# Expert stage of an attention-plus-MoE layer: explicit program order, other stage distances, and the residual moved between engines

## The chip, the cores and the metric

The kernel runs on one core of one Trainium2 chip. A core has five engines with their own instruction queues: PE (TensorE, matrix multiplies and transposes, writes to PSUM), DVE (VectorE), ACT (ScalarE), POOL (GpSimd, which also issues the indirect DMAs) and SP (SyncE, which here issues the plain DMAs). The metric is the device time of the whole program in microseconds (us).

## The reference, cut to what matters

```python
x = x + layernorm(attention(layernorm(x)))          # x: 16 x 512 x 128, relative positions, 16 heads
x = x + layernorm(ffn(layernorm(x)))

def ffn(x):                                         # x: 8192 tokens x 128
    logits = x @ w_router.T                         # 16 experts, one is chosen
    mask = one_hot(top_1(logits)); scores = sigmoid(logits) * mask
    masked_inputs = scores.T[:, :, None] * x        # zero where the expert wasn't chosen
    gate, up = split(masked_inputs @ gate_up_proj)  # 128 -> 2 x 256, each expert's own weights
    expert_out = (up * silu(gate)) @ down_proj      # 256 -> 128
    shared = (silu(x @ w_gate.T) * (x @ w_up.T)) @ w_down.T
    return shared + expert_out.sum(over experts)
```

All values are float32.

## The kernel before, in words

The program has two stages. The attention stage goes through 16 batches of 512 tokens in 256 steps of 16 per batch; the order of its work on each engine is written out by hand, with every instruction pinned behind the one traced before it on the same engine (the class `InOrder`, whose calls all show up in the profile as L47). One job of this stage is `route` (L566): for the batch that has just been finished it forms `pay`, a row of 133 words for each token: 128 words of the residual stream x, then the mean and the reciprocal standard deviation of x (columns D and D+1), the router's score (D+2), the expert (D+3) and the token's own number (D+4). An indirect DMA on POOL puts each row where its expert's tokens are gathered, in the DRAM tensor `rows`. `route` for batch 0 to 14 runs its wide work on POOL, and for the last batch on DVE; it is a generator, and a few of its steps are taken in each attention step.

The expert stage (from L812) takes the gathered rows in blocks of 128 tokens, all of one expert. In this run 73 blocks are processed; a conditional part at the end would process up to six more. Each block i goes through these helpers:

- `fetch(i)` (L852): SP reads the expert's number from the row and loads its weights: `gu` (256 KB, L862) and `dn` (128 KB, L864), from a pool of four buffers each. Every eight blocks it first loads the next eight blocks of rows, `xc` (L837), and POOL computes the row numbers for the output, `to` (L840).
- `turn_in(i)` (L868): DVE normalises x with the stored mean and reciprocal (L872), ACT multiplies the result with the score (L875), PE transposes both (L878), ACT copies the two transposes out of PSUM (`xT`, L880).
- `gates(i)` (L883): 16 matmuls (L889), eight with the shared weights `wgu` and eight with the expert's `gu`; each eight are four for gate and up, two chunks each. ACT takes the sigmoid of the gates (L891), DVE multiplies it by the gate (L892) and by the up half (L894), which gives `h`.
- `leave(i)` (L897): eight matmuls `po` (L904) add the shared and the expert's down product in one PSUM tile. DVE takes mean and variance (L85, L86), adds epsilon (L78), POOL takes the power -1/2 (L80, `lf_rs`), DVE normalises (L909), POOL adds the residual (L910) and issues the indirect DMA that writes the rows to the output (L912).

`run` (L917) calls `fetch(i+3)`, `turn_in(i+1)`, `gates(i)`, `leave(i-1)` in each iteration. In this stage nothing is pinned except SP's fetches: the framework's scheduler chooses the order on each engine, subject to the data. The tiles x2, xT, g, h and f have three buffers each; the gates' PSUM tile has two, `po` has two and the transposes' has two.

Of the kernel before, what the change touches and what calls it, by code (L numbers as in the profile page):

```python
# [9 lines left out]
F32 = mybir.dt.float32  # L10
I32 = mybir.dt.int32
AF = mybir.ActivationFunctionType
ALU = mybir.AluOpType
# [4 lines left out]
P = 128  # L18
S = 512
D = 128  # L20
# [10 lines left out]
FF = 256  # L31
# [19 lines left out]
def relative_attention_then_moe(  # L51
# [6 lines left out]
    nc = tc.nc  # L58
# [7 lines left out]
    ident = const.tile([P, P], F32, name="ident")  # L66
# [8 lines left out]
    def rstd_of(pool, mv, n, tag, eng, root=nc.gpsimd):  # L75

        ve = pool.tile([P, n], F32, tag=f"{tag}_ve", name=f"{tag}_ve")
        eng.tensor_scalar_add(ve, mv[:, :, 1], EPS)  # L78
        rs = pool.tile([P, n], F32, tag=f"{tag}_rs", name=f"{tag}_rs")
        root.tensor_tensor(rs, ve, mhalf[:, 0:n], ALU.pow)  # L80
        return rs

    def stats(pool, mv, src, tag, eng):
        st = pool.tile([P, 6], F32, tag=f"{tag}_st", name=f"{tag}_st")
        eng.bn_stats(st, src)  # L85
        eng.bn_aggr(mv, st)  # L86

    def own_rows(group, dma):

        tc.declare_no_dep(dma.ins, group=group, reason="rows of their own")  # L90
        tc.add_to_no_dep_group(group, dma.ins)


    with ExitStack() as actx:
# [4 lines left out]
        sp = actx.enter_context(tc.tile_pool(name="attn_small", bufs=4))  # L99
# [4 lines left out]
        pe, act, dve, sp_q, pool = (InOrder(tc, e) for e in (nc.tensor, nc.scalar, nc.vector, nc.sync, nc.gpsimd))  # L104
# [461 lines left out]
        def route(b, c0=0, c1=NC):  # L566
# [5 lines left out]
            nc_, pieces, nm = c1 - c0, slice(c0, c1), f"{b}_{c0}"  # L572
# [3 lines left out]
            rs = rstd_of(sp, mvy, nc_, "ry", dve, pool)  # L576
            if b == B - 1:
                yield
            pay = bp.tile([P, nc_, PW], F32, tag="pay", name=f"pay{nm}")
            pint = pay.bitcast(I32)  # L580
            mv = sp.tile([P, nc_, 2], F32, tag="mv1", name=f"mv1_{nm}")
# [13 lines left out]
            rs1 = rstd_of(sp, mv, nc_, "l1", dve, pool)  # L595
# [3 lines left out]
            for t in range(nc_):  # L599
                eng.tensor_scalar(  # L600
                    x2[:, t, :], pay[:, t, 0:D], mv[:, t, 0:1], rs1[:, t : t + 1], ALU.subtract, ALU.mult
                )
            pool.tensor_copy(pay[:, :, D : D + 1], mv[:, :, 0:1])
            pool.tensor_copy(pay[:, :, D + 1 : D + 2], rs1.unsqueeze(2))
            yield
            x2T = bp.tile([P, nc_ * P], F32, tag="x2T", name=f"x2T{nm}", bufs=1)
# [205 lines left out]
    with ExitStack() as fctx:  # L812
        wp = fctx.enter_context(tc.tile_pool(name="ffn_w", bufs=1))
        xp = fctx.enter_context(tc.tile_pool(name="ffn_x", bufs=1))
        ep = fctx.enter_context(tc.tile_pool(name="ffn_e", bufs=4))
        fp = fctx.enter_context(tc.tile_pool(name="ffn", bufs=3))
        sp = fctx.enter_context(tc.tile_pool(name="ffn_small", bufs=4))
        ps_g = fctx.enter_context(tc.tile_pool(name="ps_g", bufs=2, space=PSUM))
        ps_x = fctx.enter_context(tc.tile_pool(name="ps_x", bufs=2, space=PSUM))
        ps_f = fctx.enter_context(tc.tile_pool(name="ps_f", bufs=2, space=PSUM))  # L820

        wgu = wp.tile([P, 2 * FF], F32, name="wgu")
        wd = wp.tile([P, 2, D], F32, name="wd")
        nc.scalar.dma_start(wgu[:, 0:FF], w_gateT)
        nc.scalar.dma_start(wgu[:, FF : 2 * FF], w_upT)
        nc.scalar.dma_start(wd, w_downT.rearrange("(c p) o -> p c o", p=P))


        starts = [0, 2] + list(range(8, SURE, 8)) + [SURE, NBLK]
        rows_v = rows.rearrange("(n p) w -> p n w", p=P)  # L830
        row_of = {}
        ids_of = {}

        def fetch_rows(c):
            n0, n1 = starts[c], starts[c + 1]
            xc = xp.tile([P, n1 - n0, PW], F32, name=f"xc{c}")
            st["fetched"] = nc.sync.dma_start(xc, rows_v[:, n0:n1, :]).ins  # L837

            to = xp.tile([P, n1 - n0], I32, name=f"to{c}")
            nc.gpsimd.tensor_scalar(  # L840
                to.unsqueeze(2), xc[:, :, D + 4 : D + 5].bitcast(I32), -1.0, float(FAR), ALU.mult, ALU.add
            )
            for n in range(n0, n1):
                row_of[n] = xc[:, n - n0, :]
                ids_of[n] = to[:, n - n0 : n - n0 + 1]

        out_rows = out.rearrange("b s d -> (b s) d")
        gate_up_v = gate_up.rearrange("e p f -> p e f")
        down_v = down.rearrange("e (c p) o -> p e c o", p=P)
        st = {}  # L850

        def fetch(i):  # L852

            for c in range(2, len(starts) - 2):
                if starts[c - 1] == i:
                    with tc.issue_after(st["fetched"]):
                        fetch_rows(c)
            x = row_of[i]
            with tc.issue_after(st["fetched"]):
                e = nc.sync.value_load(x[0:1, D + 3 : D + 4].bitcast(I32), min_val=0, max_val=NE - 1)  # L860
            gu = ep.tile([P, 2 * FF], F32, tag="gu", name=f"gu{i}")
            nc.sync.dma_start(gu.unsqueeze(1), gate_up_v[:, bass.ds(e, 1), :])  # L862
            dn = ep.tile([P, 2, D], F32, tag="dn", name=f"dn{i}")
            last = nc.sync.dma_start(dn.unsqueeze(1), down_v[:, bass.ds(e, 1), :, :])  # L864
            st["fetched"] = last.ins
            st[i] = {"x": x, "gu": gu, "dn": dn}

        def turn_in(i):  # L868

            x = st[i]["x"]  # L870
            x2 = fp.tile([P, 2, D], F32, tag="x2", name=f"x2b{i}")
            nc.vector.tensor_scalar(  # L872
                x2[:, 0, :], x[:, 0:D], x[:, D : D + 1], x[:, D + 1 : D + 2], ALU.subtract, ALU.mult
            )
            nc.scalar.mul(x2[:, 1, :], x2[:, 0, :], x[:, D + 2 : D + 3])  # L875
            pt = ps_x.tile([P, 2, P], F32, tag="x", name=f"ptb{i}")
            for k in range(2):
                nc.tensor.transpose(pt[:, k, :], x2[:, k, :], ident)  # L878
            xT = fp.tile([P, 2, P], F32, tag="xT", name=f"xTb{i}")
            nc.scalar.copy(xT, pt)  # L880
            st[i]["xT"] = xT

        def gates(i):  # L883

            xT = st[i]["xT"]
            pg = ps_g.tile([P, 2, 4, P], F32, tag="g", name=f"pg{i}")
            for k, w in enumerate((wgu, st[i]["gu"])):
                for c in range(4):
                    nc.tensor.matmul(pg[:, k, c, :], w[:, c * P : (c + 1) * P], xT[:, k, :], start=True, stop=True)  # L889
            g = fp.tile([P, 2, 2, P], F32, tag="g", name=f"g{i}")  # L890
            nc.scalar.activation(g, pg[:, :, 0:2, :], AF.Sigmoid)  # L891
            nc.vector.tensor_mul(g, g, pg[:, :, 0:2, :])  # L892
            h = fp.tile([P, 2, 2, P], F32, tag="h", name=f"h{i}")
            nc.vector.tensor_mul(h, g, pg[:, :, 2:4, :])  # L894
            st[i]["h"] = h

        def leave(i):  # L897

            s = st.pop(i)
            x, h = s["x"], s["h"]  # L900
            po = ps_f.tile([P, D], F32, tag="f", name=f"po{i}")
            for k, w in enumerate((wd, s["dn"])):
                for c in range(2):
                    nc.tensor.matmul(po, h[:, k, c, :], w[:, c, :], start=(k == c == 0), stop=(k == c == 1))  # L904
            mv = sp.tile([P, 1, 2], F32, tag="mvf", name=f"mvf{i}")
            stats(sp, mv[:, 0, :], po, "lf", nc.vector)
            rs = rstd_of(sp, mv, 1, "lf", nc.vector)
            f = fp.tile([P, D], F32, tag="f", name=f"f{i}")
            nc.vector.tensor_scalar(f, po, mv[:, 0, 0:1], rs, ALU.subtract, ALU.mult)  # L909
            nc.gpsimd.tensor_add(f, f, x[:, 0:D])  # L910
            to = ids_of[i]
            own_rows("out", nc.gpsimd.indirect_dma_start(  # L912
                out_rows, bass.IndirectOffsetOnAxis(ap=to, axis=0), f, None,
                bounds_check=B * S - 1, oob_is_err=False,
            ))

        def run(i0, i1):  # L917

            for i in range(i0, min(i0 + 3, i1)):
                fetch(i)  # L920
            turn_in(i0)
            for i in range(i0, i1 + 1):
                if i + 3 < i1:
                    fetch(i + 3)
                if i + 1 < i1:
                    turn_in(i + 1)
                if i < i1:
                    gates(i)
                if i > i0:
                    leave(i - 1)  # L930

        for c in range(2):
            fetch_rows(c)
        run(0, SURE)

        opened = nc.values_load(blocks[0:1, 0:1], min_val=1, max_val=NBLK)
        with tc.If(opened > SURE):
            fetch_rows(len(starts) - 2)
            run(SURE, NBLK)
# [31 lines left out]
```

## Time and profile before

| | |
|---|---|
| three timed runs | 1972.97, 1973.37, 1974.53 us (median 1973.37) |
| the profiled execution | 1977.44 us, of which the span of instructions is 1975.7 us |
| busy over the span | PE 1905.7 us (96%), DVE 1539.5 (78%), ACT 1154.3 (58%), POOL 901.3 (46%) |
| mean granted clock of PE | 0.989 of full speed |
| attention stage | 0 to about 1730 us of the span |
| expert stage | about 1735 us to the end; last indirect DMA issued at 1970.32 us |

A page of the profile lists busy time for each engine, 40 slices of the span, the chain of work that ended last, and groups of equal instructions with their mean duration and with the idle time of their engine just before them, together with what ended that idle time. The timeline lists instructions in order of time. Each line starts with start and duration in us. "Busy" of PE counts the modelled ends of pipelined matmuls, so a PE that is always busy need not be issuing at its highest rate.

### The profile page before, as it was taken

Reading aid. Unit: us, or ns where it says so; the run is one execution under the profiler, and the core shown is the slowest. Engines: PE = TensorE matmul, PEld = TensorE weight load, DVE = VectorE, ACT = ScalarE, POOL = GpSimd, SP = SyncE. Lnnn points to the kernel's source line nnn. Section 1 sums busy time; section 2 is a strip of 40 time slices with the busy share of each in tenths; the row PEclk is TensorE's granted clock in tenths of the full one; section 3 lists DMA queues with packets and bytes.
Section 4 is the critical chain, followed back from the end, with each engine's and each line's share of the span. In section 5 each row is a group of like instructions: output and inputs, shape, how many; then the busy total and the mean of one; then the engine's idle time right before and its main releaser. Section 6 shows DMA issues by size and latency. Waiting matters only on the chain.

```text
span 1975.7 us, 92844 instructions
## 1 busy us (share of the span) xinstructions
PE 1905.7 (96%) x41070; PEld 1518.6 (77%) x41070; DVE 1539.5 (78%) x3922; ACT 1154.3 (58%) x2929; POOL 901.3 (46%) x1007
## 2 busy tenths in 40 slices
PE   6999999999999999999999999999999999689997
PEld 3777777777777777777777777777777777589997
DVE  4677787888787878787878888787878787757776
ACT  3666566666656666666666666666666666234432
POOL 4234454444444453535453544444444534246666
PEclk9999999999999999999999999999999999889999
DMA  2312000000000000000000000000000000066553
GB/s 75 69 30 42 14 23 5 14 14 6 22 5 24 5 23 3 25 3 25 3 25 3 25 3 16 12 12 16 5 18 5 18 7 5 13 176 176 173 165 95
DMA packets 88342, 68.94 MB, mean 35 GB/s; under 512 B 26439, under 2 KB 74340, under 8 KB 87808
## 3 DMA queue, kind: packets, MB, share of 16 engines
q1 hardware_dynamic: 81248, 53.60, 10.5%
q0 software_dynamic: 4384, 8.57, 1.2%
q8 instruction: 323, 5.29, 1.1%
q10 hardware_dynamic: 2304, 0.80, 0.2%
q14 instruction: 83, 0.68, 0.1%
HBM read 44.79 MB, written 18.75 MB: 32 GB/s over the span
## 4 chain that ended last, share of the span: by engine, by line
PE 80%; POOL 8%; DVE 6%; issue 5%; ACT 1%; DMA 1%; POOLq 0%; ACTq 0%; DVEq 0%; SPq 0%
PE ps L47 27%; PE pt L47 24%; PE pa L47 13%; PE pz L47 7%; POOL out_dram L912 4%; DVE nmax L47 3%; POOL lf_rs L80 2%; PE prt L47 2%; PE py L47 2%; POOL f L910 2%; PE pq L47 1%; PE pl L47 1%; PE pv L47 1%; PE pk L47 1%; DVE wT L47 1%
## 5 line engine op out<-in xcount | busy, mean ns | idle before, releaser
L47 ACT ACTIVATE w<-ps,nmax 128x512 f32<-128x512 f32 x1024 | 699.3, 693 | 497.7 <-DVE nmax L47 497.7
L47 DVE TENSOR_REDUCE nmax<-ps 128x1 f32<-128x512 f32 x1024 | 656.2, 683 | 288.3 <-PE ps L47 288.3
L47 PE MATMUL pt<-ident,w 128*128 128x128 f32 x4096 | 590.8, 280 | 3.1 <-DVE wT L47 2.7
L47 PEld LDWEIGHTS pt<-ident,w 128*128 128x128 f32 x4096 | 446.5, 141 | 139.0 <-issue 98.7
L47 ACT COPY wT<-pt 128x512 f32<-128x512 f32 x512 | 299.9, 586 | 129.0 <-PE pt L47 129.0
L47 DVE COPY wT<-pt 128x512 f32<-128x512 f32 x512 | 349.3, 682 | 1.6 <-PE pt L47 1.5
L47 PE MATMUL ps<-kT,qb 32*128 32x288 f32 (+10 forms) x4864 | 327.1, 375 | 5.4 <-POOL qb L47 3.8
L47 PE MATMUL pa<-wT,v 128*32 128x128 f32 x8192 | 276.7, 276 | 2.0 <-ACT R L47 1.2
L47 PE MATMUL ps<-relk,qr 64*32 64x288 f32 (+4 forms) x8192 | 275.2, 377 | 0.0
L47 PEld LDWEIGHTS ps<-kT,qb 32*128 32x128 f32 x4864 | 208.9, 186 | 62.9 <-issue 35.3
L47 PEld LDWEIGHTS pa<-wT,v 128*32 128x32 f32 x8192 | 208.0, 109 | 44.3 <-issue 41.6
L47 POOL TENSOR_TENSOR Rh<-R,mh 128x512 f32<-128x512 f32 x64 | 66.5, 1039 | 357.7 <-ACT R L47 351.2
L47 ACT ACTIVATION_READ_ACCUMULATOR w<-ps,nmax 128x1 f32 x1024 | 212.5, 208 | 0.0
L47 PEld LDWEIGHTS ps<-relk,qr 64*32 64x32 f32 x8192 | 124.4, 106 | 112.8 <-issue 82.8
L47 PE MATMUL pz<-wT,relv 128*32 128x48 f32 (+1 forms) x12288 | 192.1, 210 | 1.3 <-issue 1.3
L47 PEld LDWEIGHTS pz<-wT,relv 128*32 128x32 f32 x12288 | 184.1, 110 | 1.9 <-issue 1.9
L47 POOL TENSOR_TENSOR qr<-qz,mq 128x1024 f32<-128x1024 f32 x64 | 137.7, 2152 | 0.0
L47 POOL TENSOR_SCALAR kT<-kT,kend 128x512 f32<-128x512 f32 x32 | 49.8, 1562 | 145.0 <-ACT sg L47 128.3
L47 DVE TENSOR_REDUCE oT<-od 128x32 f32<-128x128 f32 x256 | 97.6, 381 | 8.9
L875 ACT ACTIVATE x2b<-x2b,xc 128x128 f32<-128x128 f32 x73 | 29.0, 401 | 125.2 <-DVE lf_ve L78 114.0
L47 POOL COPY rb<-rt 128x512 f32<-128x512 f32 x64 | 39.0, 609 | 116.6 <-DVE rt L47 104.7
L47 POOL DMA_INDIRECT rows<-pay,at_i x64 | 68.0, 1062 | 51.9 <-DVE shift L47 41.4
(157 smaller groups left out, 2241.8 us busy)
## 6 DMA issues: line engine op xcount, KB each, us to landing
gu<-_L_ffn_gate_up_proj_dram SPq DMA_DIRECT2D x73, 256.0 KB
dn<-in_L_ffn_down_proj_dram SPq DMA_DIRECT2D x73, 128.0 KB
rows<-zero SPq DMA_DIRECT2D x19, 266.0 KB
xc<-rows SPq DMA_DIRECT2D x8, 532.0 KB
x_sb<-in_L_attn_x_dram SPq DMA_DIRECT2D x64, 64.0 KB
qd<-qp SPq DMA_DIRECT2D x16, 256.0 KB
qz<-qd SPq DMA_DIRECT2D x248, 16.0 KB
relv<-vext SPq DMA_DIRECT2D x1, 1536.0 KB
```

The costliest lines, as they stand in the source:

```text
L47: return lambda *a, **k: self.tc.keep_in_program_order(op(*a, **k))
L80: root.tensor_tensor(rs, ve, mhalf[:, 0:n], ALU.pow)
L875: nc.scalar.mul(x2[:, 1, :], x2[:, 0, :], x[:, D + 2 : D + 3])
L910: nc.gpsimd.tensor_add(f, f, x[:, 0:D])
L912: own_rows("out", nc.gpsimd.indirect_dma_start(out_rows, bass.IndirectOffsetOnAxis(ap=to, axis=0), f, None, bounds_check=B * S - 1, oob_is ...
```

## The change

The edits lie in the expert stage, except for one in `route`.

- Every PE, ACT, DVE and POOL instruction of the helpers is now pinned in program order, with the same class as in the attention stage. SP's loads and the small POOL instruction `to` stay as they were.
- `route` stores minus mean times reciprocal in column D, computed by DVE, where POOL copied the mean.
- `norm(i)` is a helper of its own. ACT does both its instructions: x times the reciprocal plus column D, and then the product with the score.
- `gates(i)` orders its 16 matmuls as the gates of both layers first and the ups after them; the PSUM tile is laid out the same way, so the eight gates lie together. The two products are in `product(i)`.
- The down product, its statistics and the POOL power are in `down_proj(i)`, called two blocks behind the gates. `leave(i)`, called three behind, has DVE form `nm` (minus mean times reciprocal), ACT form x plus `nm` (`xb`), DVE form po times the reciprocal plus `xb` (f), and POOL issue the output DMA. The separate POOL addition is gone.
- The weights' pool has six buffers and the working tiles have four.
- The order of an iteration is: fetch(i+3), leave(i-3), turn_in(i+1), norm(i+2), gates(i), product(i), down_proj(i-2).

```diff
@@ -600,7 +600,9 @@
                 eng.tensor_scalar(
                     x2[:, t, :], pay[:, t, 0:D], mv[:, t, 0:1], rs1[:, t : t + 1], ALU.subtract, ALU.mult
                 )
-            pool.tensor_copy(pay[:, :, D : D + 1], mv[:, :, 0:1])
+            dve.scalar_tensor_tensor(
+                pay[:, :, D : D + 1], mv[:, :, 0:1], -1.0, rs1.unsqueeze(2), ALU.mult, ALU.mult
+            )
             pool.tensor_copy(pay[:, :, D + 1 : D + 2], rs1.unsqueeze(2))
             yield
             x2T = bp.tile([P, nc_ * P], F32, tag="x2T", name=f"x2T{nm}", bufs=1)
@@ -812,12 +814,13 @@
     with ExitStack() as fctx:
         wp = fctx.enter_context(tc.tile_pool(name="ffn_w", bufs=1))
         xp = fctx.enter_context(tc.tile_pool(name="ffn_x", bufs=1))
-        ep = fctx.enter_context(tc.tile_pool(name="ffn_e", bufs=4))
-        fp = fctx.enter_context(tc.tile_pool(name="ffn", bufs=3))
+        ep = fctx.enter_context(tc.tile_pool(name="ffn_e", bufs=6))
+        fp = fctx.enter_context(tc.tile_pool(name="ffn", bufs=4))
         sp = fctx.enter_context(tc.tile_pool(name="ffn_small", bufs=4))
         ps_g = fctx.enter_context(tc.tile_pool(name="ps_g", bufs=2, space=PSUM))
         ps_x = fctx.enter_context(tc.tile_pool(name="ps_x", bufs=2, space=PSUM))
         ps_f = fctx.enter_context(tc.tile_pool(name="ps_f", bufs=2, space=PSUM))
+        pe, act, dve, pool = (InOrder(tc, e) for e in (nc.tensor, nc.scalar, nc.vector, nc.gpsimd))
 
         wgu = wp.tile([P, 2 * FF], F32, name="wgu")
         wd = wp.tile([P, 2, D], F32, name="wd")
@@ -865,52 +868,70 @@
             st["fetched"] = last.ins
             st[i] = {"x": x, "gu": gu, "dn": dn}
 
-        def turn_in(i):
+        def norm(i):
 
             x = st[i]["x"]
             x2 = fp.tile([P, 2, D], F32, tag="x2", name=f"x2b{i}")
-            nc.vector.tensor_scalar(
-                x2[:, 0, :], x[:, 0:D], x[:, D : D + 1], x[:, D + 1 : D + 2], ALU.subtract, ALU.mult
-            )
-            nc.scalar.mul(x2[:, 1, :], x2[:, 0, :], x[:, D + 2 : D + 3])
+            act.activation(x2[:, 0, :], x[:, 0:D], AF.Identity, bias=x[:, D : D + 1], scale=x[:, D + 1 : D + 2])
+            act.mul(x2[:, 1, :], x2[:, 0, :], x[:, D + 2 : D + 3])
+            st[i]["x2"] = x2
+
+        def turn_in(i):
+
             pt = ps_x.tile([P, 2, P], F32, tag="x", name=f"ptb{i}")
             for k in range(2):
-                nc.tensor.transpose(pt[:, k, :], x2[:, k, :], ident)
+                pe.transpose(pt[:, k, :], st[i]["x2"][:, k, :], ident)
             xT = fp.tile([P, 2, P], F32, tag="xT", name=f"xTb{i}")
-            nc.scalar.copy(xT, pt)
+            act.copy(xT, pt)
             st[i]["xT"] = xT
 
         def gates(i):
 
             xT = st[i]["xT"]
-            pg = ps_g.tile([P, 2, 4, P], F32, tag="g", name=f"pg{i}")
-            for k, w in enumerate((wgu, st[i]["gu"])):
-                for c in range(4):
-                    nc.tensor.matmul(pg[:, k, c, :], w[:, c * P : (c + 1) * P], xT[:, k, :], start=True, stop=True)
+            pg = ps_g.tile([P, 2, 2, 2, P], F32, tag="g", name=f"pg{i}")
+            for u in range(2):
+                for k, w in enumerate((wgu, st[i]["gu"])):
+                    for c in range(2):
+                        a = u * FF + c * P
+                        pe.matmul(pg[:, u, k, c, :], w[:, a : a + P], xT[:, k, :], start=True, stop=True)
             g = fp.tile([P, 2, 2, P], F32, tag="g", name=f"g{i}")
-            nc.scalar.activation(g, pg[:, :, 0:2, :], AF.Sigmoid)
-            nc.vector.tensor_mul(g, g, pg[:, :, 0:2, :])
+            act.activation(g, pg[:, 0], AF.Sigmoid)
+            st[i].update(pg=pg, g=g)
+
+        def product(i):
+
+            pg, g = st[i]["pg"], st[i]["g"]
+            dve.tensor_mul(g, g, pg[:, 0])
             h = fp.tile([P, 2, 2, P], F32, tag="h", name=f"h{i}")
-            nc.vector.tensor_mul(h, g, pg[:, :, 2:4, :])
+            dve.tensor_mul(h, g, pg[:, 1])
             st[i]["h"] = h
 
-        def leave(i):
-
-            s = st.pop(i)
-            x, h = s["x"], s["h"]
+        def down_proj(i):
+
+            s = st[i]
+            h = s["h"]
             po = ps_f.tile([P, D], F32, tag="f", name=f"po{i}")
             for k, w in enumerate((wd, s["dn"])):
                 for c in range(2):
-                    nc.tensor.matmul(po, h[:, k, c, :], w[:, c, :], start=(k == c == 0), stop=(k == c == 1))
+                    pe.matmul(po, h[:, k, c, :], w[:, c, :], start=(k == c == 0), stop=(k == c == 1))
             mv = sp.tile([P, 1, 2], F32, tag="mvf", name=f"mvf{i}")
-            stats(sp, mv[:, 0, :], po, "lf", nc.vector)
-            rs = rstd_of(sp, mv, 1, "lf", nc.vector)
+            stats(sp, mv[:, 0, :], po, "lf", dve)
+            s.update(po=po, mv=mv)
+            s["rs"] = rstd_of(sp, mv, 1, "lf", dve, pool)
+
+        def leave(i):
+
+            s = st.pop(i)
+            x, po, rs = s["x"], s["po"], s["rs"]
+
+            nm = sp.tile([P, 1], F32, tag="nm", name=f"nm{i}")
+            dve.scalar_tensor_tensor(nm, s["mv"][:, :, 0], -1.0, rs, ALU.mult, ALU.mult)
+            xb = fp.tile([P, D], F32, tag="xb", name=f"xb{i}")
+            act.activation(xb, x[:, 0:D], AF.Identity, bias=nm)
             f = fp.tile([P, D], F32, tag="f", name=f"f{i}")
-            nc.vector.tensor_scalar(f, po, mv[:, 0, 0:1], rs, ALU.subtract, ALU.mult)
-            nc.gpsimd.tensor_add(f, f, x[:, 0:D])
-            to = ids_of[i]
-            own_rows("out", nc.gpsimd.indirect_dma_start(
-                out_rows, bass.IndirectOffsetOnAxis(ap=to, axis=0), f, None,
+            dve.scalar_tensor_tensor(f, po, rs, xb, ALU.mult, ALU.add)
+            own_rows("out", pool.indirect_dma_start(
+                out_rows, bass.IndirectOffsetOnAxis(ap=ids_of[i], axis=0), f, None,
                 bounds_check=B * S - 1, oob_is_err=False,
             ))
 
@@ -918,16 +939,23 @@
 
             for i in range(i0, min(i0 + 3, i1)):
                 fetch(i)
+            norm(i0)
+            norm(i0 + 1)
             turn_in(i0)
-            for i in range(i0, i1 + 1):
+            for i in range(i0, i1 + 3):
                 if i + 3 < i1:
                     fetch(i + 3)
+                if i0 <= i - 3 < i1:
+                    leave(i - 3)
                 if i + 1 < i1:
                     turn_in(i + 1)
+                if i + 2 < i1:
+                    norm(i + 2)
                 if i < i1:
                     gates(i)
-                if i > i0:
-                    leave(i - 1)
+                    product(i)
+                if i0 <= i - 2 < i1:
+                    down_proj(i - 2)
 
         for c in range(2):
             fetch_rows(c)
```

## The prediction

> **What bounds the kernel now.** I read the slices of the page first, then the stage table, the timeline of single blocks, and the rows of the groups. The columns of the stage table are the stretch and its length, then busy time (and instructions) of PE, weight loads, DVE, ACT, POOL, then clock, DMA share and GB/s.
>
> ```profile
> PE   6999999999999999999999999999999999689997
> DVE  4677787888787878787878888787878787757776
> ...
> 1800.00:1840.00 40.00, 39.54 (x341) 38.72 (x340) 30.03 (x92) 16.41 (x40) 26.90 (x42) 1.00 0.62 178
> ```
>
> PE looks full everywhere, but the row hides a small gap: 341 matmuls in 40 us are 117 ns each, and where PE really runs back to back, 26 of them (2 transposes, 16 gates and ups, 8 down) take 2.90 us (block starts at 1747.32, 1750.21, 1753.11), 111.5 ns each. Most blocks take 3.02 us. The timeline of DVE and POOL for one of them says why; the bracket at the end is idle time and its releaser.
>
> ```profile
> 1818.00 0.68 DVE L892 TENSOR_TENSOR g<-g,pg 128x512 f32<-128x512 f32 x1
> 1818.60 0.29 DVE L85 BATCH_NORM_STATS2 lf_st<-po 128x6 f32<-128x128 f32 x1
> 1818.81 0.67 DVE L894 TENSOR_TENSOR h<-g,pg 128x512 f32<-128x512 f32 x1
> 1819.39 0.17 DVE L86 BATCH_NORM_AGGREGATE mvf<-lf_st 128x2 f32<-128x6 f32 x1
> 1819.48 0.49 DVE L872 TENSOR_SCALAR x2b<-xc 128x128 f32<-128x128 f32 x1
> 1819.71 0.27 DVE L78 TENSOR_SCALAR lf_ve<-mvf 128x1 f32<-128x1 f32 x1
> 1820.70 0.41 DVE L909 TENSOR_SCALAR f<-po,mvf,lf_rs 128x128 f32<-128x128 f32 x1 [0.72 <-POOL lf_rs L80]
> ...
> 1818.91 1.03 POOL L912 DMA_INDIRECT out_dram<-f,to  x1 [0.29 <-POOL f L910]
> 1820.10 0.57 POOL L80 TENSOR_TENSOR lf_rs<-lf_ve,mhalf 128x1 f32<-128x1 f32 x1 [0.15 <-DVE lf_ve L78]
> 1821.19 0.46 POOL L910 TENSOR_TENSOR f<-f,xc 128x128 f32<-128x128 f32 x1 [0.53 <-DVE f L909]
> ```
>
> It is a closed round over two engines: f starts at 1820.70, POOL's addition .49 later, the output DMA .74 after that (1821.93), the next power 1.19 later (1823.12), the next f .60 later: .49 + .74 + 1.19 + .60 = 3.02. PE's floor of 2.90 lies only .12 below, so removing this round altogether is worth 73 x .12 = 8.8 us, or 0.45% of the kernel.
>
> **The change, part by part.** The three things it removes from the old round are real: POOL loses the addition (.43 a block), DVE loses L872 (pitch .23), and PE finds h finished two blocks earlier. In busy time no engine is over 2.9 us a block afterwards. But with every engine pinned as written, I have to follow the order, not the sum. It is safe to take the order literally: the attention stage uses the same pinning, and there DVE runs nmax twice, wT, nmax twice, od, oT, wT, just as its loop is written. In an iteration i the queues hold
>
> DVE: nm(i-3), f(i-3), g(i), h(i), then statistics, aggregate and epsilon of i-2.
> POOL: output DMA(i-3), power(i-2). ACT: xb(i-3), xT(i+1), the two norm instructions (i+2), sigmoid(i). PE: transposes(i+1), gates(i), down(i-2).
>
> The epsilon of i-2 is DVE's last instruction of an iteration, and nm(i-2), which needs POOL's power of it, is the first of the next. The whole DVE queue waits there. Then xb waits for nm at the head of ACT's queue; behind it stand xT, both norm instructions and the sigmoid, and DVE's g waits for that sigmoid. So the distances of two and three blocks hide nothing: one round per block goes through nm, xb, sigmoid, g, h, statistics, power, nm. Its terms, start to start:
>
> - nm on 128x1: .16 (scalar_tensor_tensor on 128x16 took .17, the epsilon .15), and .04 until ACT starts (DVE to ACT at 1716.93 to 1716.97): .20.
> - xb, as L875 .40 long, followed at a pitch of .31 (L875 at 1817.05, sigmoid at 1817.36): .31. xT .37 long, pitch .25 to .31: .28.
> - First norm instruction, two pointer operands, which no row shows. With one pointer L875 took .401. The price of a pointer is in the trace too:
>
> ```profile
> L47 ACT ACTIVATE w<-ps,nmax 128x512 f32<-128x512 f32 x1024 | 699.3, 693 | 497.7 <-DVE nmax L47 497.7
> L891 ACT ACTIVATE g<-pg 128x512 f32<-128x512 f32 x73 | 42.3, 580 | 12.6 <-PE pg L889 10.5 <-DVE mvf L86 2.1
> ```
>
>   693 with a bias pointer against 580 without, .11. Bounds .40 (second pointer free) and .51; I take .48, and .03 until the dependent second norm instruction may start (g to h, .68 long, are .71 apart): .51.
> - Second norm instruction, pitch .31. Sigmoid .58 and .03 until g (1747.00 to 1747.03): .61.
> - g to h .71 (with the statistics between, it was .81). h to statistics .59 (h at 1818.81, next at 1819.39). Statistics to aggregate .33, to epsilon .21 (1966.50, 1966.83, 1967.04). Epsilon .15 and .08 until POOL starts (1717.49 to 1717.57): .23. Power .57 and .04: .61.
>
> The sum is .20 + .31 + .28 + .51 + .31 + .61 + .71 + .59 + .33 + .21 + .23 + .61 = **4.90 us** a block against 3.02. What lies beside it: f (ends 1.04 after nm, g starts at 2.22); the output DMA (f's end + .3, then 1.03 and .15: POOL is free at 2.5, the power starts at 4.3); PE, which needs about 3.0 of 4.9 and runs ahead (gates(i) need xT(i), copied one iteration before, and h(i-2)); and down(i-2), done well before the statistics ask for it. f costs nothing only as long as the sigmoid is later; without that cover it stands .35 in the round.
>
> Moved DMA work: the output DMA now trails one more block, once, at the end. SP's queue keeps its order; six weight buffers let it run two blocks further ahead, at 384 KB in 4.9 us instead of 3.02, so no weights are late. POOL's `to` waits for rows xc; now every later POOL instruction is pinned behind it. SP issues xc about an iteration ahead of that (landing took some 5 us at 1739.55 to 1744.57), so each of the nine chunks costs between 0 and 2 us, the lower end being nearer: 0.
>
> **The edit in route.** DVE now waits for POOL's power l_rs right behind l_ve. At 929.26 l_ve ran for .16, the power from 929.51 to 930.55, so the new instruction (.17) ends near 930.76. DVE was idle anyway:
>
> ```profile
> 930.87 1.29 DVE L47 TENSOR_REDUCE nmax<-ps 128x1 f32<-128x512 f32 x2 [1.45 <-PE ps L47]
> ```
>
> PE's scores hide it, with .1 to spare, and the same 1.45 stands behind l_ve in 14 of 15 batches (1.39 in the last of them). Without that cover it would be at most 15 x .2 = 3 us; I take 0. In the last batch two such instructions stand on the chain: .3.
>
> **The sum.** The first nm comes at about 1747.5 (rows ready 1735.1; two blocks' norm .9 each on ACT, xT(0), 16 cold matmuls from 1737.2 to 1740.9 as before; two more blocks of gates; statistics and power of block 0). Then 68 full rounds, 68 x 4.90 = 333.2; one without norm, 4.08; one without norm and xT, 3.80; two without gates, bound by DMA then power, 3.1 each; last nm near 2094.8. Its f and DMA issue end 2.40 later, and the span ends 4.35 after that, as before (1971.35 to 1975.7): 2101.6, with .3 from route **2102** against a span of 1975.7, +126. The profiled execution took 1977.44, 4 above the median of the runs; I add the difference to the median: 1973.4 + 126 = **2099.4 us**, 6.4% slower.
>
> **Rule against row: the clock.** PE will be idle about 1.9 us in every 4.9. The Trainium skill (TensorE: Matmul & The Clock Gate, "The HAM clock gate") has the clock halve only after an idle window of some 3.4 us; by that rule nothing changes. The trace is stricter:
>
> ```profile
> 1902.00:1904.00 2.00, 0.00 (x0) 0.00 (x0) 1.57 (x4) 0.00 (x0) 1.14 (x3) 1.00 0.89 215
> 1904.00:1906.00 2.00, 1.72 (x12) 1.72 (x13) 1.28 (x6) 1.00 (x3) 1.32 (x3) 0.85 0.73 249
> 1906.00:1908.00 2.00, 2.00 (x12) 2.00 (x11) 1.76 (x6) 0.40 (x2) 1.68 (x4) 0.50 0.35 86
> ```
>
> A gap of only 2.3 us was followed by some 3 us at half clock. At half clock a block is 26 x 223 ns = 5.80, which would then set the pace: +.90 x 68 = +61 us if it held throughout. It can't hold easily, as PE would be always busy and return to full speed, as it did at 1908; and a slow phase of 3 us costs PE 1.5, within its slack. I take 0 and keep 0 to +30.
>
> **Rivals.**
> 1. ACT is not in the round (the sigmoid gets past xb, or is early enough): nm, xb, f, g, h and the rest are .20 + .43 + .30 + .71 + .59 + .33 + .21 + .23 + .61 = 3.61, 68 x 1.29 = 88 less: 2011 us. Against it: xb is called before gates.
> 2. The other side: the queues don't wait as written, and PE's floor is the pace. 2.90 a block: 2099 - 68 x 2.00 = 1963 us, faster. It decides as soon as the round is under 2.90; the terms would have to be wrong by 2.00, which only the power and the sigmoid chain both leaving the round would give. For it speaks only that busy times all fit under 2.9.
> 3. The change does not do what it says (the scheduler's order differs although pinned, and the old round comes back): 1973, no change.
> 4. Half clock or waits for `to` in many rounds: 2130 to 2160.
>
> **How the numbers follow.** The 4.90 round has 0.80, rival 1 0.07, rival 2 0.03, rival 3 0.02, rival 4 0.08. The likeliest one's own range: the two-pointer instruction .40 to .51, twelve handovers and pitches each uncertain by about .03, so 4.6 to 5.2 a block, -20 to +20 us: 2079 to 2120. The 8-in-10 range reaches from there towards rival 1 and into rival 4: 2050 to 2135. Faster by over 0.2% (the spread of the runs shown is 0.08%, so about what can be told from no change) has 0.03, within it 0.02, slower 0.95.
>
> **What would show it.** Right: nm preceded by about .7 idle released by lf_rs; xb released by nm; g preceded by over 1 us released by ACT's g; PE's slices in the last stage near 6, waits of PE for x2b; attention ends at the same time. Wrong: output DMAs less than 4.5 us apart (a term left the round), PE's clock below .9 with matmuls of twice the length (rival 4), `nmax` later than before behind l_ve (the route edit is not hidden), or an ACT table load in each block, which the 2 loads of the whole run speak against: one set served Exp and Identity.

## The result, and the profile after

The changed kernel takes **2116.8 us** (2113.6 to 2117.7, four runs) against 1974.0 us before (1973.0 to 1976.7): a ratio of **1.071**, 95% interval 1.070 to 1.073. The forecast was 2099 us, with a range of 2050 to 2135.

The slices of the page and the stage table of the changed kernel (in the second: stretch, length, then busy time and instructions of PE, weight loads, DVE, ACT, POOL, then clock, DMA share, GB/s):

```profile
PE   6999999999999999999999999999999957677765
DVE  4777878787878787878787878787878755444444
```

```profile
1840.00:1880.00 40.00, 28.28 (x208) 25.13 (x208) 19.42 (x56) 15.58 (x41) 13.01 (x17) 0.96 0.37 107
```

Up to slice 32, in the attention stage, the rows are as full as before (a slice is 52.8 us here, 49.4 before). In the expert stage every engine has become idler: 208 matmuls in 40 us where there were 341, and no engine is over 71% busy. That is what a closed round over several engines looks like. The timeline of DVE, for one block:

```profile
1834.69 0.16 DVE L47 SCALAR_TENSOR_TENSOR nm<-mvf,lf_rs 128x1 f32<-128x1 f32 x1 [0.88 <-POOL lf_rs L47]
1835.32 0.35 DVE L47 SCALAR_TENSOR_TENSOR f<-po,lf_rs,xb 128x128 f32<-128x128 f32 x1 [0.47 <-ACT xb L47]
1836.88 0.69 DVE L47 TENSOR_TENSOR g<-g,pg 128x512 f32<-128x512 f32 x1 [1.22 <-ACT g L47]
1837.60 0.69 DVE L47 TENSOR_TENSOR h<-g,pg 128x512 f32<-128x512 f32 x1
1838.21 0.29 DVE L47 BATCH_NORM_STATS2 lf_st<-po 128x6 f32<-128x128 f32 x1
1838.53 0.18 DVE L47 BATCH_NORM_AGGREGATE mvf<-lf_st 128x2 f32<-128x6 f32 x1
1838.75 0.15 DVE L47 TENSOR_SCALAR lf_ve<-mvf 128x1 f32<-128x1 f32 x1
1839.66 0.16 DVE L47 SCALAR_TENSOR_TENSOR nm<-mvf,lf_rs 128x1 f32<-128x1 f32 x1 [0.76 <-POOL lf_rs L47]
```

The same round on ACT, on POOL, and on PE:

```profile
1834.88 0.40 ACT L47 ACTIVATE xb<-xc,nm 128x128 f32<-128x128 f32 x1 [3.12 <-DVE nm L47]
1835.19 0.35 ACT L47 COPY xTb<-ptb 128x256 f32<-128x256 f32 x1
1835.44 0.49 ACT L47 ACTIVATE x2b<-xc 128x128 f32<-128x128 f32 x1
1835.97 0.40 ACT L47 ACTIVATE x2b<-x2b,xc 128x128 f32<-128x128 f32 x1
1836.27 0.58 ACT L47 ACTIVATE g<-pg 128x512 f32<-128x512 f32 x1
...
1839.06 0.57 POOL L47 TENSOR_TENSOR lf_rs<-lf_ve,mhalf 128x1 f32<-128x1 f32 x1 [2.04 <-DVE lf_ve L47]
...
1840.96 0.76 PE L47 MATMUL ptb<-ident,x2b 128*128 128x128 f32 x2 [1.52 <-ACT x2b L47]
```

nm to nm is 4.97 us (forecast 4.90). DVE stands still three times in it, for the power, for xb and for the sigmoid; ACT sleeps 3 us until nm; PE ends its block and waits 1.5 us for ACT. Each start is released by the one before it in the round, across the engines. Both signs that the forecast named are here: g stands idle for 1.22 us until ACT's g, and PE's transposes wait for x2b.

The edit in `route` cost nothing. On DVE in the attention stage the new instruction waits for POOL, in time that was idle before:

```profile
928.47 0.16 DVE L47 TENSOR_SCALAR l_ve<-mv 128x4 f32<-128x4 f32 x1
929.79 0.17 DVE L47 SCALAR_TENSOR_TENSOR pay<-mv,l_rs 128x4 f32<-128x4 f32 x1 [1.17 <-POOL l_rs L47]
930.07 1.29 DVE L47 TENSOR_REDUCE nmax<-ps 128x1 f32<-128x512 f32 x2
```

nmax follows l_ve by 1.60 us, as before (929.26 to 930.87), and the last nmax of the stage starts at 1692.1, where it was 1692.3.

### The profile page after: what moved, and what is told of

Read it like the earlier page. It is cut to its first block, busy times and chain, and to the rows that moved or that the text cites. A ratio compares the mean times of both kernels' runs of the same rounds, so it can differ in the third digit from the quotient of the medians.

```text
span 2111.6 us, 92975 instructions
## 1 busy us (share of the span) xinstructions
PE 1939.4 (92%) x41070; PEld 1529.8 (72%) x41070; DVE 1549.0 (73%) x3939; ACT 1204.2 (57%) x3075; POOL 867.5 (41%) x917
## 5 line engine op out<-in xcount | busy, mean ns | idle before, releaser
L47 ACT ACTIVATE xb<-xc,nm 128x128 f32<-128x128 f32 x73 | 29.3, 401 | 221.3 <-DVE nm L47 221.3
L47 PE MATMUL ptb<-ident,x2b 128*128 128x128 f32 x146 | 48.0, 335 | 111.9 <-ACT x2b L47 105.0
L47 DVE TENSOR_TENSOR g<-g,pg 128x512 f32<-128x512 f32 x73 | 50.2, 687 | 98.4 <-ACT g L47 98.2
L47 PEld LDWEIGHTS ptb<-ident,x2b 128*128 128x128 f32 x146 | 20.8, 143 | 138.1 <-ACT x2b L47 137.7
L47 POOL DMA_INDIRECT out_dram<-f,to x73 | 75.8, 1038 | 97.6 <-DVE f L47 92.2
```

Source lines behind the costliest of these rows:

```text
L47: return lambda *a, **k: self.tc.keep_in_program_order(op(*a, **k))
```

## The experiments

The theory: the written order closes a round per block through nm, xb, sigmoid, g, h, statistics and power. The rivals: (A) the distances and instructions cost by themselves, (B) only POOL's power is exposed and ACT is beside the round, (C) the distance covers the power, (D) PE or its clock sets the pace. Some kernels (e5, e6, e7 and the three split versions) ran on another chip, where the kernel before takes 1989 to 1990 us and the first row numbers of the expert stage come 13 to 20 us later than in the changed kernel's trace; between the chips I therefore compare the length of a round, read as the distance between equal instructions of successive blocks. e1 to e9 have one time each, so no interval is given for them.

**The order alone: e1.** Everything of the change except the pinning.

```diff
-        pe, act, dve, pool = (InOrder(tc, e) for e in (nc.tensor, nc.scalar, nc.vector, nc.gpsimd))
+        pe, act, dve, pool = nc.tensor, nc.scalar, nc.vector, nc.gpsimd
```

> The changed kernel with the pinning of the expert stage taken off; calls, distances and instructions stay. In the built program the scheduler now puts ACT's xb behind the sigmoid of its iteration, and DVE's nm ahead of g, with f between g and h. My theory (the written order closes one round per block through nm, xb, sigmoid, g, h, statistics, power): the sigmoid chain leaves the round, what stays is nm, g, f, h, statistics, aggregate, epsilon, power: .13 + .60 + .30 + .60 + .33 + .22 + .23 + .61 = 3.0 us a block, about 1975 to 1982 us. Rival A (the distances of two and three blocks or the instructions themselves are slow, whatever the order): stays near 2115 us.

Measured: 1980.0 us beside 1973.2 for the kernel before, 2.99 us a block. DVE's timeline:

```profile
1850.72 0.16 DVE L928 SCALAR_TENSOR_TENSOR nm<-mvf,lf_rs 128x1 f32<-128x1 f32 x1 [0.76 <-POOL lf_rs L80]
1850.80 0.68 DVE L904 TENSOR_TENSOR g<-g,pg 128x512 f32<-128x512 f32 x1
1851.40 0.34 DVE L932 SCALAR_TENSOR_TENSOR f<-po,lf_rs,xb 128x128 f32<-128x128 f32 x1
```

The wait for the power is as long as ever, but g no longer waits for ACT, and f finds xb ready. Nearly the whole loss is in the order: rival A falls. What is left, DVE with the power in it, gives the round of 3.0 us that was forecast.

**The other half: e9.** The kernel before with the pinning alone, in its own call order.

```diff
+        pe, act, dve, pool = (InOrder(tc, e) for e in (nc.tensor, nc.scalar, nc.vector, nc.gpsimd))
# and in turn_in, gates, leave: nc.vector -> dve, nc.scalar -> act, nc.tensor -> pe, nc.gpsimd -> pool
```

> The kernel before with nothing but the pinning: its own call order turn_in(i+1), gates(i), leave(i-1) on PE, ACT, DVE and POOL of the expert stage. It separates the pinning from the new distances. My theory: what costs is the written order closing rounds, and this one closes a longer one: x2 on DVE .39, ACT .43, transposes .22, sixteen matmuls 1.95, sigmoid .66, g .72, h .61, statistics .33, aggregate .22, epsilon .31, power .60, f .32: 6.8 us a block, about + 270 us on the kernel before, more if PE's clock falls at 43% of use. Rival A (the new distances and instructions are what costs): about as before, within 10 us.

Measured: 2339.4 us beside 1974.9. This order is far worse than the changed kernel's, so the new distances and instructions together helped a pinned kernel; they didn't hide enough. Three rounds in the trace took 6.7 us, as the sum says, but most took 7.9 to 8.5. The stage table and PE's timeline say why:

```profile
1900.00:2040.00 140.00, 90.26 (x440) 83.27 (x440) 43.92 (x119) 23.30 (x51) 35.60 (x53) 0.71 0.23 68
```

```profile
1854.79 0.87 PE L47 MATMUL ptb<-ident,x2b 128*128 128x128 f32 x2 [3.19 <-DVE x2b L47]
1855.45 1.91 PE L47 MATMUL pg<-xTb,wgu 128*128 128x128 f32 x8
1857.16 1.91 PE L47 MATMUL pg<-xTb,gu 128*128 128x128 f32 x8
```

Eight matmuls take 1.91 us instead of 1.06: the clock is at half, with a mean of .71. Sixteen matmuls at half the clock are 1.7 us more, which takes a round of 6.7 to 8.4. Here PE lies in the round, idles 2.5 to 3.3 us in each, and pays for it.

**Which part of the order: e2, e3, e4.** Each takes one piece out of the round.

```diff
# e2: leave(i - 3) moved down            # e3: one block later            # e4
-   leave(i - 3)  # ahead of turn_in     -   leave(i - 3)                 -   act.activation(xb, x[:, 0:D], AF.Identity, bias=nm)
    product(i)                           +   leave(i - 4)                 +   pool.tensor_scalar_add(xb, x[:, 0:D], nm)
+   leave(i - 3)                         # and one more iteration
    down_proj(i - 2)
```

> The changed kernel with leave(i-3) called behind product(i) and ahead of down_proj(i-2); still pinned. My theory: the power gets the whole of g and h as cover and leaves the round; the ACT chain stays: nm to g 2.19 (as measured in the changed kernel), g to h .72, h to nm .60: 3.51 us a block, 2117 - 68 x 1.46 = about 2018 us. Rival B (only the wait for POOL's power is exposed, ACT is not in the round): the round falls to about PE's pace of 2.9 to 3.0, some 1970 to 1980 us.

> The changed kernel with leave(i-4) at the place of leave(i-3), so one block more of distance and the same order on the engines; still pinned. My theory: only the power leaves the round, epsilon to nm falls from .91 to .10: 4.97 - .81 = 4.16 us a block, 2117 - 68 x .81 + one more iteration of 3 = about 2064 us. Rival B: some 1970 to 1980 us. Rival A: 2117 us or more.

> The changed kernel with xb = x + nm computed by POOL instead of ACT; order and distances stay. My theory: the sigmoid no longer stands behind nm; nm to g falls from 2.19 to .24 + .45 to .79 for POOL's addition + .04 + .30 for f = 1.0 to 1.4: a round of 3.8 to 4.2 us, about 2040 to 2062 us, and g no longer waits for ACT. Rival B: ACT is not in the round, xb's time only moves to a slower engine: 2117 us or a little more.

Measured: e2 2014.0 us (round 3.52), e3 2052.2 us (4.13), e4 2044.4 us (3.94); the kernel before beside them 1973.2. On DVE, in e2:

```profile
1851.03 0.69 DVE L47 TENSOR_TENSOR g<-g,pg 128x512 f32<-128x512 f32 x1 [0.61 <-ACT g L47]
1851.75 0.69 DVE L47 TENSOR_TENSOR h<-g,pg 128x512 f32<-128x512 f32 x1
1852.36 0.15 DVE L47 SCALAR_TENSOR_TENSOR nm<-mvf,lf_rs 128x1 f32<-128x1 f32 x1
```

In e3:

```profile
1852.10 0.15 DVE L47 TENSOR_SCALAR lf_ve<-mvf 128x1 f32<-128x1 f32 x1
1852.17 0.15 DVE L47 SCALAR_TENSOR_TENSOR nm<-mvf,lf_rs 128x1 f32<-128x1 f32 x1
...
1854.35 0.69 DVE L47 TENSOR_TENSOR g<-g,pg 128x512 f32<-128x512 f32 x1 [1.22 <-ACT g L47]
```

In e4:

```profile
1850.40 0.16 DVE L47 SCALAR_TENSOR_TENSOR nm<-mvf,lf_rs 128x1 f32<-128x1 f32 x1 [0.76 <-POOL lf_rs L47]
1851.30 0.35 DVE L47 SCALAR_TENSOR_TENSOR f<-po,lf_rs,xb 128x128 f32<-128x128 f32 x1 [0.74 <-POOL xb L47]
1851.57 0.68 DVE L47 TENSOR_TENSOR g<-g,pg 128x512 f32<-128x512 f32 x1
```

In e2 and e3 nm follows without a wait: one block of distance, or g and h in between, hides the power, worth .84 us (4.97 to 4.13). The ACT chain remains in both, and g waits for it. In e4 it is the other way round: the power is still there, g's wait for ACT is gone, worth 1.03 with POOL's longer xb already taken off. Rival B is out, as it had e2 and e3 near 1975. e3's time came 12 us under the expected one although its round was met within .03. The sum had added an iteration at the start and still counted 68 full rounds, where the trace has 67 (4.1 us); a round fell by .85, not .81 (some 2.5); and it began from the changed kernel's median, 3.2 above its profiled execution, which itself holds 3.1 us of waits that e3 lacks (the next section has them).

**One cost doubled: e5 and e6.**

```diff
# e5, in down_proj
-            s["rs"] = rstd_of(sp, mv, 1, "lf", dve, pool)
+            once = rstd_of(sp, mv, 1, "lf", dve, pool)
+            pool.tensor_tensor(s["rs"], once, mone, ALU.pow)        # mone holds 1.0; s["rs"] a tile of its own
# e6, in gates
-            for u in range(2):
+            for u in (0, 0, 1):
```

> The changed kernel with a second POOL power (exponent one) behind the first, so nm waits for two of them. My theory: the power lies in the round with its full length: + .57 and .03 a block, 72 x .60 = +43, about 2160 us. Rival C (the block distance covers the power, the time goes elsewhere): no change.

> The changed kernel with the eight gate matmuls of each block done twice over, into the same place: 34 matmuls a block instead of 26, 3.8 us at full clock. My theory: PE has 2 us of slack in a round of 4.97: no change, within 6 us. Rival D (PE at a reduced clock or PE's order sets the pace): + .9 x 73 = +65 us, about 2180 us.

Measured: e5 2166.7 us, a round of 5.53, .56 more, about the power's own length: it is fully exposed, and C is out. On DVE, nm's wait has grown from .76 to 1.31:

```profile
1843.12 0.16 DVE L47 SCALAR_TENSOR_TENSOR nm<-mvf,again 128x1 f32<-128x1 f32 x1 [1.31 <-POOL again L47]
```

e6 took 2128.6 us on the chip where the kernel before takes 1989, a round of 4.975, no change, with eight more matmuls in each. PE's timeline in e6 shows only a smaller gap:

```profile
1843.52 0.76 PE L47 MATMUL ptb<-ident,x2b 128*128 128x128 f32 x2 [0.64 <-ACT x2b L47]
```

So D is out for the changed kernel. Its clock does dip: around 1908, in the changed kernel, four matmuls take 1.06 us for .61, and the round there is 4.98 (nm at 1904.46 and 1909.44). PE is beside the round, and a dip lands in its slack. In e6, with gaps of .64, the clock was 1.00 in every stretch of 50 us from 1800 to 2100.

**What was off in the sum: e7 and e8.** In the changed kernel the first sigmoid came late. PE's and ACT's timelines:

```profile
1737.36 1.21 PE L47 MATMUL pg<-xTb,wgu 128*128 128x128 f32 x4
1738.55 1.22 PE L47 MATMUL pg<-xTb,gu 128*128 128x128 f32 x4
1739.56 1.06 PE L47 MATMUL pg<-xTb,wgu 128*128 128x128 f32 x4
1740.42 1.06 PE L47 MATMUL pg<-xTb,gu 128*128 128x128 f32 x4
...
1741.51 0.60 ACT L47 ACTIVATE g<-pg 128x512 f32<-128x512 f32 x1 [2.72 <-PE pg L47]
```

The gates are the first eight, done near 1739.8; the sigmoid starts when all 16 have ended.

```diff
# e7, in gates
-            pg = ps_g.tile([P, 2, 2, 2, P], F32, tag="g", name=f"pg{i}")
+            pg = [ps_g.tile([P, 2, 2, P], F32, tag=t, name=f"{t}{i}") for t in ("pg", "pu")]
# e8
-        sp = fctx.enter_context(tc.tile_pool(name="ffn_small", bufs=4))
+        sp = fctx.enter_context(tc.tile_pool(name="ffn_small", bufs=80))
```

> The changed kernel with gates and ups of a block in two PSUM tiles. Theory: in the changed kernel the first sigmoid waited for all 16 matmuls, though the gates alone were done after the first 8; with two tiles it starts about 2 us earlier in the first block, and nm of block 0 comes 1 to 2.5 us earlier behind the first row numbers than the 14.9 us of the changed kernel. The rounds stay at 4.97, since there the sigmoid waits for its turn on ACT. If the late start had another cause, the 14.9 us stay.

> The changed kernel with 80 instead of 4 buffers for the small tiles (statistics, epsilon, power, nm), so that none is used twice. In the changed kernel the first three rounds took 4.91 us and all later ones 4.97, and POOL's power started .16 behind the end of the epsilon instead of .08 to .09. Theory: from the fifth block on the power's tile is a reused buffer, and the power waits for a second event (the reader of the old contents), long past, whose handling costs .06 to .07: here all rounds take 4.91. If the extra time has another cause: 4.97 from the fourth round on, as before.

Measured for e7: the first sigmoid 4.9 us behind the first row numbers instead of 6.4, the first nm 14.0 instead of 14.9: the wait was for the tile as a whole. The gain at nm, .9, is just under the 1 to 2.5 that were expected: what leads to the first nm is the sigmoid of the third block, by when PE runs at full clock and eight matmuls take .9. The rounds did not stay: 5.04 instead of 4.97, since h now follows g by .79 instead of .72. That it has a second set of matmuls to wait for, long done, is the likely reason; no run separates it. The time, 2138.4 us beside 1990.3, includes two rounds of 6.7.

Measured for e8: 2109.2 us beside 1974.9; rounds of 4.91 throughout (apart from those with a wait for rows), and epsilon to power back from .31 to .25:

```profile
1844.05 0.15 DVE L47 TENSOR_SCALAR lf_ve<-mvf 128x1 f32<-128x1 f32 x1
1844.30 0.57 POOL L47 TENSOR_TENSOR lf_rs<-lf_ve,mhalf 128x1 f32<-128x1 f32 x1 [2.01 <-DVE lf_ve L47]
```

So reuse of the small buffers costs .06 to .07 a round.

**A version from the theory: w1, w3, w2.** `leave` is split: nm(i-4) first on DVE, xb(i-4) behind the sigmoid on ACT, f(i-4) and the DMA last.

```diff
-                if i0 <= i - 3 < i1:
-                    leave(i - 3)
+                if i0 <= i - 4 < i1:
+                    shift_of(i - 4)          # dve: nm
                 turn_in(i + 1); norm(i + 2); gates(i)
+                residual(i - 4)              # act: xb
-                product(i)                   # g, h
+                product(i)                   # w1: g, h    w3 and w2: g alone here
                 down_proj(i - 2)
+                leave(i - 4)                 # dve: f, then the DMA; w3 and w2: between g and h
# ps_f bufs 2 -> 3, ps_x bufs 2 -> 1; w2 also has e7's two PSUM tiles
```

> A version made from the theory: pinned as in the changed kernel, leave split in three and four blocks behind: nm(i-4) first on DVE, xb(i-4) on ACT behind the sigmoid of i, f(i-4) last on DVE behind the epsilon of i-2, then the output DMA; po with three buffers and the transposes with one. My theory: no closed round is left but each engine's own work: DVE .10 + .72 + .60 + .33 + .22 + .10 + .33 = 2.4, ACT 2.0, POOL 1.8, so PE's 2.90 is the pace, against 3.02 and some stalls before: 1963 us (1958 to 1969), ratio to before 0.995. Rival E (something else, as DMA or POOL, holds the pace near 3.02): 1971 to 1978 us.

Measured for w1: 1997.6 us against 1989.1, ratio 1.005 (1.003 to 1.006): a miss. Rounds of 2.91 and 3.28 alternate. The timeline shows the long one, with DVE's f and the weight load of the down product (PEld) among PE's lines:

```profile
1843.48 0.61 PE L47 MATMUL pg<-xTb,gu 128*128 128x128 f32 x4
1843.82 0.35 DVE L47 SCALAR_TENSOR_TENSOR f<-po,lf_rs,xb 128x128 f32<-128x128 f32 x1
1844.22 0.52 PEld L47 LDWEIGHTS po<-wd,h 128*128 128x128 f32 x4 [0.32 <-DVE f L47]
1844.22 0.71 PE L47 MATMUL po<-wd,h 128*128 128x128 f32 x4
1844.77 0.61 PE L47 MATMUL po<-dn,h 128*128 128x128 f32 x4
```

Sets of four follow each other at .45; the down product comes at .74. It waits for f on DVE, which is last in its iteration and ends at 1844.17: f is the last to read the po buffer that the product needs.

> As w2, but with gates and ups in one PSUM tile, as the changed kernel has them. Theory: if the sigmoid's late start (behind all 16 matmuls) leaves enough slack, this has the same 2.90 a block and the two differ by at most 2 us; if the late start is what made every second round long, rounds of 2.9 and 3.3 alternate here as before, about + 12 us against w2.

> The split version again, with f(i-4) between g and h, and with gates and ups of a block in two PSUM tiles of one bank each. In the split version two waits were left: the sigmoid started only when all 16 matmuls of gates had ended (1844.13, the last four from 1843.48), and the down product waited for a buffer of po until f, late on DVE, had read it (.3 in every second block). My theory: both go, and PE's own 2.90 a block is the pace: 72 rounds of 2.90 to 2.93 instead of an average of 3.09 before, less 12 us, plus 1 to 3 for a longer start and drain: ratio to before 0.995 (0.993 to 0.997). Rival E (the pace is held near 3.0 by something else, as POOL or the loads): 0.998 to 1.005.

Measured: w3 1983.3 us, ratio 0.997 (0.996 to 0.998); w2 **1980.2 us against 1990.3, ratio 0.995 (0.994 to 0.997)**. Both have rounds of 2.90: from the first h to the last w2 takes 208.6 us and w3 208.2, where the kernel before, on its own chip, takes 222.0. The two tiles start the sigmoid some .7 us earlier in the block (1.31 us behind the first gate matmul instead of 1.98) and change the pace by nothing, and the intervals of the two overlap. The stage table of w2:

```profile
1820.00:1860.00 40.00, 40.00 (x361) 40.00 (x361) 30.08 (x98) 26.58 (x70) 22.17 (x29) 1.00 0.59 174
```

361 matmuls in 40 us are 110.8 ns each, PE's own rate, with every other engine below. So w2 is faster than the kernel before, by 10.1 us or half a percent, near the 8.8 us that the prediction gave for removing the old round; it was timed beside it, and not beside the changed kernel. Both versions are pinned like the changed kernel: so pinning need not cost anything; the order that it fixes did.

## Why the prediction was right

**Point by point.** The round, the floor and the hidden `route` edit were as forecast. The terms of the round against what was measured in the block shown above: nm to xb .20 and .19; xb to xT .31 and .31; xT .28 and .25; first norm instruction .51 and .53; second .31 and .30; sigmoid .61 and .61; g to h .71 and .72; h to statistics .59 and .61; to aggregate .33 and .32; to epsilon .21 and .22; epsilon to power **.23 and .31**; power to nm .61 and .60. The other eleven differ by at most .03 and cancel, so the 4.90 came close by its terms and not by luck. The norm instruction with two pointer operands took .49, near the .48 taken between the bounds of .40 and .51. The runs that take ACT or the power out of the round (e4, e2, e3) gave the rounds worked out for them from the changed kernel's trace before they ran. The rule on the clock and the row differ in e9: the Trainium skill (TensorE: Matmul & The Clock Gate, "The HAM clock gate") names an idle window of about 3.4 us, and gaps of 2.5 to 3.3 us with 8 us rounds already gave a mean clock of .71. In the changed kernel, with gaps of 1.5, it stayed at .97 to .99 in five of seven stretches of 50 us; it was .93 in one and .86 in that from 1900 on, below the .9 that the forecast had named as a sign of rival 4. It didn't matter, as forecast, because PE is beside the round.

**Where the sum was 17.4 us short** (2116.8 against 2099.4):
- The start, 2.5 us (first nm at 1750.0, not 1747.5). The forecast let the sigmoid start behind the gates; it waits for all 16 matmuls. e7 shows the wait, and .9 us of this. Of the rest, PE begins the second block .5 later than in the kernel before (transposes at 1741.27 and 1740.74), and eight of its matmuls still take 1.57 us for .90; what is left was not traced.
- The round, 4.9 in 68: the first three took 4.91, the others 4.975. The term is epsilon to power, which the forecast had read from `route` (1717.49 to 1717.57). It is longer from the fifth use of a set of four buffers on; e8 shows that the reuse makes it.
- POOL's `to`, taken as 0 of a bound of 0 to 2 us for each of nine: 3.1 us in six rounds of the profiled execution, 2.15 of it in one, just beyond the bound, where POOL stood behind rows that came late and held back a power already released:

```profile
1910.71 1.03 POOL L47 DMA_INDIRECT out_dram<-f,to  x1 [1.30 <-DVE f L47]
1915.80 0.20 POOL L843 TENSOR_SCALAR to<-xc 128x8 int32<-128x8 int32 x1 [4.06 <-DMA xc<-rows]
1915.96 0.57 POOL L47 TENSOR_TENSOR lf_rs<-lf_ve,mhalf 128x1 f32<-128x1 f32 x1
```

- The end, .5 us less than forecast, and the .3 for `route`, which didn't show (row numbers at 1735.14, and 1735.11 before). Together 9.7 on the span: 2111.6 against 2102.
- The step from span to median, 7.7. The forecast took the profiled execution as 4 us above the median, as in the kernel before. Here it took 2113.6 us, 2.0 above its span, and is the fastest of four; the others have spans of 2114 to 2116. That longer waits for rows make the difference is likely, since e7 has two such rounds, but there is no trace of these three, and it is not shown.

## What to carry to other kernels

In a pinned pipeline, don't count blocks of distance; write down each engine's queue for one iteration and look for a round that returns to its start one iteration later. A value made at the end of one queue's iteration and used at the head of the next has a distance of one instruction, whatever the block numbers say, and it drags in all that stands behind its user on the next engine. To break the round, put the user behind work that doesn't need it, as w3 does with nm, xb and f, and then check what holds the buffers: the piece moved late is the one that frees them.

## What the runs showed of the hardware that was not expected

- Reusing a buffer cost .06 to .07 us on POOL, from the fifth use of four buffers on (4.91 to 4.97 a round, gone in e8), and reading a tile of its own cost h as much on DVE (.72 to .79 behind g, in e7). A further wait on the instruction, for an event long past, would explain both; that is inferred.
- One pointer operand more on ACT took .09 us (.401 to .493 at 128 columns).
- With idle gaps of 2.5 to 3.3 us in rounds of about 8 us, PE's mean clock was .71. A gap of 1.53 us (before 1905.76, in the changed kernel) was also followed by some 3 us at half clock. How often that happens differs between nearly equal rounds: .86 to .99 in stretches of 50 us in the changed kernel, .80 to .94 in stretches of 40 us and more in e7, .83 to .90 in e5, and 1.00 from 1800 to 2100 in e6, where the gaps are .64. The runs don't show what decides it; e5 and e7 ran on another chip than the changed kernel, but so did e6.
